# Summing a scan's states two at a time instead of four, and moving the gate multiply one scan later

## The chip, the cores and the metric

The kernel runs on one core of a Trainium2 chip. The metric is the device time of one execution in microseconds (us). The engines named below work from queues of their own and in order: PE (TensorE, matrix multiplies; PEld is its weight load), DVE (VectorE), ACT (ScalarE), POOL (GpSimd), and SP, which only issues DMAs.

## What is computed

The model has two layers over 8 sequences of 1024 positions with 256 features. The first is a mixture of experts, causal attention, and the mixture again. The second is a channel mix, a selective state-space scan, and the channel mix again. The change lies in the scan, cut here to what matters (512 inner channels `d`, 16 states `n`):

```
deltaA   = exp(delta * A)                       # [b, d, t, n]
deltaB_u = delta * B * u                        # [b, d, t, n]
state[t] = deltaA[t] * state[t-1] + deltaB_u[t]
y[t]     = sum over n of state[t, n] * C[t, n]
y        = (y + u * D) * silu(z)
out      = y @ out_proj.T + x
```

## The kernel before

The first layer ends at about 2920 us; from there to about 5470 us the scans of the second layer run (method `run` of class `Layer1`).

**Scans.** A tile has 128 partitions: 16 channels by 8 states. So one scan covers 16 channels, 8 of the 16 states and all 1024 positions. A sequence takes 64 scans: four blocks `c` of 128 channels, and in each block 8 groups of 16 channels (`l`), each in two halves `p` of the states. `order` lists all 512 scans; the main loop takes one in each turn, `i` counts them, and `k = i % 16` is the place in the block. The groups `l` are taken in the order 0, 2, 4, 6, 1, 3, 5, 7.

**One turn of the loop.** ACT makes the decays of the next scan into the tile `h` (L1648, `decay`), from data that SP's DMAs have spread over the states (`sdl`, L1616). POOL makes the input of the scan after the next (L1639, `feed`). DVE runs the scan (L1740), then multiplies by C into a tile `hc` (L1745). There are two buffers of `h`, so the decays of scan i+1 wait until `hc` of scan i-1 is made.

**The sum over states.** `add_up` lets PE sum over the 8 states of each channel, by multiplying `hc` with a matrix `pick` of zeros and ones (L1665). One group of 16 channels fills 16 columns; `pick` has 32 columns, so that two groups share a strip of 32 output partitions of the PSUM tile `y`. Consecutive groups in the order above lie in different strips: group `l` goes to strip `l // 2`. One scan takes two matmul instructions, one for each half of the positions (`t0`). `add_up` is called before scans 4, 8, 12, ... and takes the four `hc` tiles that have gathered: two groups, in two strips, with both halves of the states each. Inside a call the order is by `t0`, then by half `p`, then by scan.

**The end of a block.** In turn k = 1 of the next block `close` lets DVE add `u * D` to `y` (L1676, the tile `uc`) and POOL multiply by silu(z) (L1679, the tile `zs`). There is one `y` tile, so the first `add_up` of a block waits until L1676 has read the last one.

**Side work.** Between the scans, `side.turn(0.5)` is called twice a turn, and each call takes steps from generators by due times that are worked out when the program is built: `steps_before` (layer norm, channel mix, input projection and convolution of the next sequence), `steps_low` and `steps_delta`, `steps_gate` (silu(z)), and `steps_behind` (output projection and channel mix of the sequence before). Their matmuls are `tr` (L1228), `pk` (L1264), `pr` (L1286), `pv` (L1304), `pc` (L1391), `px` (L1421), `pu` (L1442), `pd` (L1459) and `pp` (L1524). ACT and DVE take the results out of PSUM in the same queues in which the decays and scans stand. The order on every engine is fixed by the order of the calls.

Of the kernel before, what the change touches and what calls it, by code (L numbers as in the profile page):

```python
# [40 lines left out]
NS = 16  # L41
# [1020 lines left out]
class Layer1:  # L1062
# [10 lines left out]
    NP = 8  # L1073
    G = P // NP
    PARTS = NS // NP
    Q = 4
    RG = 32
    AHEAD = 4

# [517 lines left out]
    def run(self, pools, load, load_x, keep_x, store):  # L1597
        net, nc = self.net, self.net.nc
        T, W, B = net.T, self.W, net.B
        seqs = [self.Sequence(b) for b in range(B)]  # L1600

        lines = [l for j in range(self.RG // self.G)
                 for l in range(j, P // self.G, self.RG // self.G)]
        order = [
            (b, c, l, p) for b in range(B) for c in range(NDC) for l in lines
            for p in range(self.PARTS)
        ]
        spread, inputs, decays, summed = {}, {}, {}, []

        def fetch(i):  # L1610

            if i < len(order):
                b, c, l, p = order[i]
                for name, src in (("dl", seqs[b].steps[c]), ("du", seqs[b].du[c])):
                    spread[name, i] = t = pools["s" + name].tile([P, T], F32, name="s" + name)
                    nc.sync.dma_start(  # L1616
                        t,
                        src[l * self.G : (l + 1) * self.G, :].unsqueeze(1).to_broadcast(
                            [self.G, self.NP, T]
                        ),  # L1620
                    )

        def rep(b, name, p):

            t = seqs[b].rep[name, p] = pools["rep"].tile([P, T], F32, name=f"{name}{p}")
            src = seqs[b].bc["bc".index(name)][p * self.NP : (p + 1) * self.NP, :]
            nc.sync.dma_start(t, src.unsqueeze(0).to_broadcast([self.G, self.NP, T]))

        def feed(i):


            if i < len(order):
                b, c, l, p = order[i]
                t = spread["du", i - p]
                inputs[i] = (
                    spread.pop(("du", i - p)) if p == self.PARTS - 1
                    else pools["dbu"].tile([P, T], F32, name="dbu")
                )
                nc.gpsimd.tensor_tensor(inputs[i], t, seqs[b].rep["b", p], ALU.mult)  # L1639
                if (c, l) == (NDC - 1, lines[-1]) and b + 1 < B:  # L1640
                    rep(b + 1, "b", p)

        def decay(i):
            if i < len(order):
                b, c, l, p = order[i]
                n = c * P // self.G + l
                decays[i] = pools["h"].tile([P, T], F32, name="h")
                nc.scalar.activation(  # L1648
                    decays[i], spread["dl", i - p], AF.Exp, scale=self.A[:, p, n : n + 1]
                )  # L1650

        def add_up():

            i0 = summed[0][0]
            b, c, _, _ = order[i0]
            first = i0 % NS == 0
            if first:
                self.py = pools["y"].tile([P, T], F32, name="y")
            for t0 in range(0, T, W):
                for p in range(self.PARTS):  # L1660
                    for i, hc in summed:
                        l, n = order[i][2:]
                        if n == p:
                            g, j = divmod(l, self.RG // self.G)
                            nc.tensor.matmul(  # L1665
                                self.py[g * self.RG : (g + 1) * self.RG, t0 : t0 + W],
                                self.pick[:, j, :], hc[:, t0 : t0 + W], start=(j == 0 and p == 0),
                                stop=(j == self.RG // self.G - 1 and p == self.PARTS - 1),
                            )
            summed.clear()  # L1670

        def close(i):

            b, c = order[i][:2]
            q = seqs[b]
            nc.vector.scalar_tensor_tensor(  # L1676
                q.uc[c], q.uc[c], self.skip[:, c : c + 1], self.py, ALU.mult, ALU.add
            )
            nc.gpsimd.tensor_tensor(q.uc[c], q.uc[c], q.zs, ALU.mult)  # L1679

        def before(b):

            q = seqs[b]
            q.room = (lambda: seqs[b - 2].out) if b > 1 else None
            return self.steps_before(
                q, pools, pipe, lambda x: load(x, b), lambda x: keep_x(x, b)
            )

        def behind(b):
            when = (lambda: seqs[b + 2].mixed) if b + 2 < B else None  # L1690
            return self.steps_behind(
                seqs[b], pools, pipe, lambda x: load_x(x, b), lambda x: store(x, b), when
            )

        self.tables()
        side, pipe = self.Steps(), self.Pipe()
        side.add("2before", before(0))
        side.drain("2before")
        side.add("2low", self.steps_low(seqs[0], pools, pipe))
        side.drain("2low")  # L1700
        for p in range(self.PARTS):
            rep(0, "b", p)
            rep(0, "c", p)
        for i in range(0, self.AHEAD, self.PARTS):
            fetch(i)
        feed(0)
        feed(1)
        decay(0)
        for i, (b, c, l, p) in enumerate(order):
            k = i % NS  # L1710
            if k == 2:
                if c == 0:
                    if b > 0:
                        side.drain("3behind")
                        side.add("3behind", behind(b - 1), 85, 56)
                    if b + 1 < B:
                        side.add("2before", before(b + 1), 175, 48)
            if k == (0 if 0 < c < NDC - 1 else 2):
                side.add(
                    "1gate", self.steps_gate(seqs[b], c, pools, pipe),  # L1720
                    *((30, 8) if c + 1 < NDC else (8, 2)),
                )
            if c == NDC - 1 and b + 1 < B and not seqs[b + 1].low:
                if k == 5:
                    side.drain("2before")
                if "2before" not in side.lists:
                    seqs[b + 1].low = True
                    side.add("2low", self.steps_low(seqs[b + 1], pools, pipe), 33, 6)
            if k == NS - self.AHEAD:
                side.drain("1gate")  # L1730
                if c == NDC - 1:
                    side.drain("2low")
            if p == 0:
                fetch(i + self.AHEAD)
            decay(i + 1)
            feed(i + 2)
            side.turn(0.5)
            if i % self.Q == 0 and i:
                add_up()
            nc.vector.tensor_tensor_scan(  # L1740
                decays[i], decays[i], inputs.pop(i), 0.0, ALU.mult, ALU.add
            )
            side.turn(0.5)
            hc = pools["hc"].tile([P, T], F32, name="hc")
            nc.vector.tensor_tensor(hc, decays.pop(i), seqs[b].rep["c", p], ALU.mult)  # L1745
            summed.append((i, hc))
            if (c, l) == (NDC - 1, lines[-1]) and b + 1 < B:
                rep(b + 1, "c", p)
            if k == 1:
                if i > 1:  # L1750
                    close(i - 2)
        side.drain("3behind")
        add_up()
        close(len(order) - 1)
        side.add("3behind", behind(B - 1))
        side.drain("3behind")

# [181 lines left out]
```

## Time and profile before

Three runs took 5544.22 to 5549.63 us, with a median of 5545.22 us.

| what | value |
|---|---|
| the profiled execution's own time | 5545.59 us |
| its span, first to last instruction | 5543.9 us |
| mean granted clock of TensorE over the span | 0.881 of full speed |
| stretch of the scans | 2924 to 5470 us, 2546 us |
| in that stretch, busy: PE | 1933.35 us |
| DVE | 1925.97 us |
| POOL | 1749.66 us |
| ACT | 1435.67 us |
| in that stretch, matmuls of `y` on PE | 674.99 us, 2048 records |

A group of the profile is all instructions of one line with one engine and one pair of tiles. Its busy time counts overlapping instructions once, and the mean counts each with its full length; where they overlap, the count times the mean is more than the busy time. A matmul of 32-bit numbers leaves two records in the trace[...].

### The profile page before, as it was taken

The page shows a single profiled execution, that of the slowest core. Times are in us where ns is not written, and L with a number is a line of the kernel's source. Part 1 is how long each engine was busy: PE and PEld are TensorE (multiplying, and loading weights), DVE is VectorE, ACT ScalarE, POOL GpSimd, SP SyncE. Part 2 cuts the span into 40 slices and gives each one's busy share as a digit, 9 for nine tenths or more (in the row PEclk, how much of TensorE's full clock was granted, in tenths as well). Part 3 has the DMA queues.
Part 4 walks back from the last instruction along what each step waited for, and adds up shares of the span by engine and source line. Part 5 has one row for each costly group of instructions (what it writes and reads, how often), then busy time and mean ns, then how long its engine had stood idle before and what let it go on. Part 6 is the DMA issues. An engine that isn't in the chain of part 4 may idle for free.

```text
span 5543.9 us, 60312 instructions
## 1 busy us (share of the span) xinstructions
PE 4501.1 (81%) x21046; PEld 2165.4 (39%) x21046; DVE 3400.8 (61%) x5590; ACT 2562.0 (46%) x4374; POOL 2388.7 (43%) x2089
## 2 busy tenths in 40 slices
PE   5699699999999998499766768788787778877767
PEld 5365434444444443265432233233333324333224
DVE  5632166666666764633107777778777777777884
ACT  2111145665566554011145646565564655646453
POOL 1244211111111111234317767667666766667773
PEclk6799889999999998699887889889898888989878
DMA  6133212212221221132205454535446464454652
GB/s 213 28 59 63 76 42 75 72 60 70 83 72 62 69 75 57 48 58 57 42 28 148 130 151 126 153 103 153 133 115 160 113 165 111 121 149 129 164 138 63
DMA packets 253570, 545.28 MB, mean 98 GB/s; under 512 B 30257, under 2 KB 144001, under 8 KB 253266
## 3 DMA queue, kind: packets, MB, share of 16 engines
q1 hardware_dynamic: 228690, 507.34, 33.1%
q0 software_dynamic: 24576, 34.10, 3.8%
q8 instruction: 166, 2.72, 0.2%
q14 instruction: 138, 1.13, 0.1%
HBM read 400.31 MB, written 141.03 MB: 98 GB/s over the span
## 4 chain that ended last, share of the span: by engine, by line
PE 23%; DVE 9%; ACT 7%; POOL 6%; issue 5%; DMA 3%; SPq 0%; DVEq 0%; POOLq 0%; ACTq 0%
DVE h L1740 6%; PE y L1665 4%; PE pc L1391 4%; PE pk L1264 3%; PE pr L1286 3%; PE pu L1442 2%; ACT h L1648 2%; DMA sdu<-du 1%; PE pp L1524 1%; POOL dbu L1639 1%; PE po L489 1%; DVE hc L1745 1%; PE px L1421 1%; ACT xn L1220 1%; PE pm L472 1%
## 5 line engine op out<-in xcount | busy, mean ns | idle before, releaser
L777 ACT ACTIVATE pT<-s 128x512 f32<-128x512 f32 (+3 forms) x1536 | 669.5, 489 | 522.9 <-PE s L734 513.7
L1665 PE MATMUL y<-hc,pick 128*32 128x512 f32 x2048 | 675.0, 739 | 280.4 <-DVE hc L1745 269.1
L734 PE MATMUL s<-kT,qT 32*128 32x512 f32 (+3 forms) x3072 | 829.9, 538 | 14.1 <-DVE mx L750 11.4
L1648 ACT ACTIVATE h<-sdl,A 128x1024 f32<-128x1024 f32 x512 | 567.6, 1113 | 510.8 <-DVE hc L1745 490.6
L1740 DVE TENSOR_TENSOR_SCAN h<-h,dbu 128x1024 f32<-128x1024 f32 x256 | 586.5, 2291 | 283.1 <-ACT h L1648 161.5
L734 PE MATMUL s<-qT,kT 32*128 32x512 f32 (+3 forms) x3072 | 743.4, 539 | 8.1 <-ACT pT L777 8.1
L1639 POOL TENSOR_TENSOR dbu<-sdu,b 128x1024 f32<-128x1024 f32 x256 | 602.5, 2354 | 284.6 <-DVE h L1740 142.0
L1740 DVE TENSOR_TENSOR_SCAN h<-h,sdu 128x1024 f32<-128x1024 f32 x256 | 586.4, 2290 | 186.6 <-ACT h L1648 149.0
L1745 DVE TENSOR_TENSOR hc<-h,c 128x1024 f32<-128x1024 f32 x512 | 626.0, 1223 | 48.1 <-DMA c<-bc 9.7
L783 POOL TENSOR_SCALAR_AFFINE_SELECT pT<-pT 128x512 f32<-128x512 f32 x256 | 162.4, 634 | 1136.5 <-ACT pT L777 1052.8
L1639 POOL TENSOR_TENSOR sdu<-sdu,b 128x1024 f32<-128x1024 f32 x256 | 602.4, 2353 | 14.8 <-DMA b<-bc 2.8
L734 PEld LDWEIGHTS s<-kT,qT 32*128 32x128 f32 x3072 | 319.6, 186 | 434.9 <-DVE mx L750 188.6
L476 ACT ACTIVATE mid<-pm,bu 128x512 f32<-128x512 f32 x192 | 131.6, 686 | 728.8 <-PE pm L472 721.3
L747 DVE TENSOR_REDUCE part<-s 128x1 f32<-128x512 f32 x512 | 329.2, 685 | 178.5 <-PE s L734 177.9
L1665 PEld LDWEIGHTS y<-hc,pick 128*32 128x32 f32 x2048 | 133.5, 127 | 774.8 <-DVE hc L1745 386.7
L497 POOL DMA_INDIRECT acc<-o,idx x128 | 210.5, 1644 | 495.5 <-DVE o L494 240.6
L750 DVE CUSTOM_DVE_ANT_0 junk<-s,mask,part 128x256 f32<-128x256 f32 (+3 forms) x512 | 281.5, 550 | 157.5 <-PE s L734 112.6
L472 PE MATMUL pm<-tT,wu 128*128 128x512 f32 x768 | 362.4, 609 | 0.0
L489 PE MATMUL po<-wd,mid 128*128 128x256 f32 x1536 | 350.4, 392 | 0.0
L750 DVE CUSTOM_DVE_ANT_0 junk<-s,mask 128x256 f32<-128x256 f32 (+3 forms) x512 | 250.5, 489 | 138.9 <-PE s L734 86.7
L797 PE MATMUL po<-pT,at_v 128*32 128x512 f32 (+3 forms) x3072 | 329.5, 501 | 0.7 <-POOL pT L783 0.4
L1442 PE MATMUL pu<-hT,w_in 128*128 128x512 f32 x512 | 269.1, 667 | 63.7 <-DVE cm_r L1310 48.7
(261 smaller groups left out, 6778.8 us busy)
## 6 DMA issues: line engine op xcount, KB each, us to landing
sdl<-dl SPq DMA_DIRECT2D x256, 512.0 KB
sdu<-du SPq DMA_DIRECT2D x256, 512.0 KB
acc<-xt SPq DMA_DIRECT2D x24, 1024.0 KB
xt<-acc SPq DMA_DIRECT2D x24, 1024.0 KB
rows<-moe_r SPq DMA_DIRECT2D x16, 1056.0 KB
qT<-padded_q SPq DMA_DIRECT2D x32, 512.0 KB
kT<-padded_k SPq DMA_DIRECT2D x32, 512.0 KB
kept<-so SPq DMA_DIRECT2D x64, 256.0 KB
```

The costliest lines, as they stand in the source:

```text
L472: nc.tensor.matmul(pm, wu[:, k, n * P : (n + 1) * P], tT[:, k, t0 : t0 + HALF], start=(k == 0), stop=(k == KC - 1),)
L489: nc.tensor.matmul(po, mid[:, n, j * P : (j + 1) * P], wd[:, n, :], start=(n == 0), stop=(n == NF - 1),)
L734: self.net.nc.tensor.matmul(s[:, 0 : rhs.shape[-1]], lhsT, rhs, start=True, stop=True)
L750: nc.vector.tensor_tensor_reduce(junk[:, 0:w], sh[:, 0:w], self.mask[:, W - w : W], 1.0, part if a else -3e38, ALU.add, ALU.max, self.mx[n ...
L777: self.net.nc.scalar.activation(pT[:, h, 0:w], sh[:, 0:w], AF.Exp, scale=1.0 / HD**0.5)
L797: nc.tensor.matmul(q.po[h * HS : (h + 1) * HS, o:W], self.va[q.b % 2][:, j, g * HG + h, :], pT[:, h, 0 : W - o], start=(j == 0), stop=(j = ...
L1442: self.net.nc.tensor.matmul(pu, self.w_in[:, k, e0 : e0 + P], q.hT[:, k, t0 : t0 + self.W], start=(k == 0), stop=(k == KC - 1),)
L1639: nc.gpsimd.tensor_tensor(inputs[i], t, seqs[b].rep["b", p], ALU.mult)
L1648: nc.scalar.activation(decays[i], spread["dl", i - p], AF.Exp, scale=self.A[:, p, n : n + 1])
L1665: nc.tensor.matmul(self.py[g * self.RG : (g + 1) * self.RG, t0 : t0 + W], self.pick[:, j, :], hc[:, t0 : t0 + W], start=(j == 0 and p == 0 ...
L1740: nc.vector.tensor_tensor_scan(decays[i], decays[i], inputs.pop(i), 0.0, ALU.mult, ALU.add)
L1745: nc.vector.tensor_tensor(hc, decays.pop(i), seqs[b].rep["c", p], ALU.mult)
```

## The change

`Q` goes from 4 to 2, so `add_up` is called at every second scan and takes the two halves `p` of one group of channels, which lie in one strip. The call stands after the scan instead of ahead of it. The multiply by silu(z) leaves `close` for a function `gated`, which is called in turn k = 2, behind the next `feed`.

```diff
-    Q = 4
+    Q = 2
...
-            i0 = summed[0][0]
-            b, c, _, _ = order[i0]
-            first = i0 % NS == 0
-            if first:
+            if summed[0][0] % NS == 0:
                 self.py = pools["y"].tile([P, T], F32, name="y")
...
+
+        def gated(i):
+            b, c = order[i][:2]
+            q = seqs[b]
             nc.gpsimd.tensor_tensor(q.uc[c], q.uc[c], q.zs, ALU.mult)
...
             feed(i + 2)
+            if k == 2 and i > NS:
+                gated(i - 3)
             side.turn(0.5)
-            if i % self.Q == 0 and i:
-                add_up()
             nc.vector.tensor_tensor_scan(
                 decays[i], decays[i], inputs.pop(i), 0.0, ALU.mult, ALU.add
             )
+            if i % self.Q == 0 and i:
+                add_up()
             side.turn(0.5)
...
         close(len(order) - 1)
+        gated(len(order) - 1)
```

## The prediction

> **What bounds the kernel.** I read the page's chain first, then the groups, and then only the stretch of the scans, by windows of four scans. The chain for the whole span:
>
> ```profile
> PE 23%; DVE 9%; ACT 7%; POOL 6%; issue 5%; DMA 3%; SPq 0%; DVEq 0%; POOLq 0%; ACTq 0%
> L1665 PE MATMUL y<-hc,pick 128*32 128x512 f32 x2048 | 675.0, 739 | 280.4 <-DVE hc L1745 269.1
> L1740 DVE TENSOR_TENSOR_SCAN h<-h,dbu 128x1024 f32<-128x1024 f32 x256 | 586.5, 2291 | 283.1 <-ACT h L1648 161.5
> ```
>
> PE leads the chain. The sums are PE's largest group of the scan stretch, and the scans themselves wait for ACT's decays, which stand in ACT's queue behind work that takes results from PE. So a late PE becomes a late scan by way of ACT.
>
> The sequences 1 to 6 repeat each other within a few us. I take sequence 3 (3871.3 to 4202.4 us) as the pattern. Six of its 16 windows (bounds and length; then busy time and count of PE, PEld, DVE, ACT, POOL; clock; DMA share and rate):
>
> ```profile
> 3871.30:3891.70 20.40, 13.68 (x29) 2.59 (x30) 17.17 (x19) 9.86 (x13) 13.60 (x7) 0.67 0.97 248
> 3930.30:3950.40 20.10, 20.10 (x79) 12.34 (x77) 13.95 (x10) 10.85 (x13) 9.44 (x4) 1.00 0.34 91
> 4048.10:4077.80 29.70, 26.62 (x86) 12.72 (x84) 15.17 (x9) 20.05 (x29) 12.15 (x12) 1.00 0.23 59
> 4097.10:4113.50 16.40, 16.40 (x57) 7.70 (x54) 14.45 (x10) 10.59 (x15) 12.00 (x7) 1.00 0.56 147
> 4130.50:4153.10 22.60, 22.29 (x60) 8.39 (x59) 15.19 (x9) 13.62 (x15) 10.62 (x6) 1.00 0.20 50
> 4173.00:4187.60 14.60, 9.25 (x24) 2.63 (x24) 13.76 (x9) 5.49 (x7) 14.44 (x9) 0.73 0.57 170
> ```
>
> Four scans need 14 us of DVE (4 x (2.29 + 1.22)). The last row is near that, and the first is filled by DVE (17.17 us) and the DMAs (share 0.97): there PE has room. In the four between, PE is busy 90 to 100% and the scans are stretched: there PE is the bound. The chain of this sequence, in order of weight, begins:
>
> ```profile
> by line: PE y L1665 10.2%; PE pc L1391 8.5%; DMA sdu<-du 7.8%; DVE h L1740 7.7%; issue 6.8%; PE pk L1264 6.8%; PE pr L1286 6.4%; PE pu L1442 4.9%; ACT h L1648 4.3%; PE pp L1524 3.9%; ACT L1156 2.3%; DMA c<-bc 2.3%; PE px L1421 2.2%; POOL db
> ```
>
> 10.2% of 331.1 us are 33.8 us of `y` on the path.
>
> **What a sum costs, paired and alone.** One call of `add_up` before, from the timeline (start, length, engine, line):
>
> ```profile
> 3599.78 3.63 PE L1665 MATMUL y<-hc,pick 128*32 128x512 f32 x16
> ...
> 3600.24 0.12 PEld L1665 LDWEIGHTS y<-hc,pick 128*32 128x32 f32 x2 [0.31 <-issue]
> 3600.66 0.12 PEld L1665 LDWEIGHTS y<-hc,pick 128*32 128x32 f32 x2 [0.31 <-issue]
> 3601.09 0.12 PEld L1665 LDWEIGHTS y<-hc,pick 128*32 128x32 f32 x2 [0.31 <-issue]
> ```
>
> 16 records (8 instructions[...]) take 3.63 us, and the weights come two at a time every 0.43 us: two matmuls run beside each other, one in the strip of each group. Alone they show where one group's second half is ready and the other's is not:
>
> ```profile
> 3835.55 0.11 PEld L1665 LDWEIGHTS y<-hc,pick 128*32 128x32 f32 x1 [0.31 <-issue]
> 3835.97 0.11 PEld L1665 LDWEIGHTS y<-hc,pick 128*32 128x32 f32 x1 [0.32 <-issue]
> ...
> 3842.01 0.19 PEld L1665 LDWEIGHTS y<-hc,pick 128*32 128x32 f32 x4 [5.92 <-DVE hc L1745]
> ```
>
> One load instead of two, at the same step of 0.42 us. A lone record costs as much as a pair. The full-width neighbour agrees: `pk` (128 columns, 512 positions) takes 3.60 us for 8 records, one after the other.
>
> With Q = 2 a call holds the two halves of one group, in one strip, adding into the same partitions: nothing is left to run beside. Each call has 4 instructions, 8 records, 8 x 0.43 = 3.43 us. Four scans then cost 6.87 us of PE instead of 3.43 us of steps. **PE gains 3.43 us of work per four scans**; x128 that is 439 us at full clock.
>
> Here a rule speaks against the change. The Trainium skill (TensorE: Matmul & The Clock Gate, Part 3, and the table "Why this matters for your kernels") says to put small-M outputs in different strips of 32 partitions so that they run concurrently, and gives 2.38x for three tiles. Scaled evenly, two tiles would gain 1.59x and losing them would cost 3.63 x 0.59 = 2.1 us per four scans, in all 274 us of PE. The row of this trace has twice the work in the same step, so I take 3.43 us and 439 us.
>
> **Part by part.**
>
> *Call behind the scan.* The call emits only PE work. The order on DVE, ACT and SP does not change; on PE the order of the side work does not either. The call stays between the same two side turns, so its move past a DVE instruction alone is worth 0. The wait is still for `hc` of scan i-1, not for scan i. If it took in scan i, the price would be up to 2.29 us in a call; I see no reason for it.
>
> *Every second scan.* In turns i = 4, 8, ... PE has a group at the same place as before, with 8 lone steps instead of 8 paired ones: 0. In turns i = 2, 6, ... there is a new group of 3.43 us between pieces of side work, which now waits for the `hc` before it. Behind it stand side matmuls, and behind these ACT's evacuations and the decays. Where PE is late, the wait is over already; where PE is early, DVE is the bound and has its inputs. Between 0 and 3.43 us per window at full clock, so I go through the windows of sequence 3 by what stands behind the new group:
>
> - Windows 1, 15, 16 (from 3871, 4173, 4188 us; DVE and DMAs bound, PE idle 5.4 to 6.7 us): 0. Window 3 (3930): the new group comes behind `pr`, whose result ACT waits for: 0 there. Window 7 (4012): only an empty gap: 0.
> - Window 2 (3892): the group falls between the transposes and `pp`, for which DVE waits 13 us: 3.4. Window 4 (3950): late by the group of window 3, `pv` comes later than DVE's read of it, which had about 0.6 us to spare: 2.8. Window 6 (3991): the group of window 5 splits `pr`, ACT's sigmoid is late, a scan waits for ACT already: 2.2. Window 8 (4028): between transposes, with `y` on the path already: 3.4.
> - Windows 9, 10, 11, 13, 14 (PE 76 to 100% busy, `pc`, `pr` or `px` behind the group): 3.4, 3.0, 3.4, 3.4, 3.4. Window 12 (PE idle 4.2 us, half usable): 2.0.
> - Window 5: -1.0 for the gate, next.
>
> Sum: 29.4 us a sequence, x6 = 176 us.
>
> *Gate multiply later.* In POOL's queue L1679 moves behind one `feed`:
>
> ```profile
> POOL uc L1679 <- DVE uc L1676: 268.9, 30, 18.6
> ```
>
> POOL stood 269 us before this multiply in total. It now feeds first. But the inputs are made two scans ahead, and POOL is idle over 30% of the stretch; on the path lie only 2.35 us, in window 5, beside an ACT branch (`pk`, `ka`, decays) nearly as long. The gain lies between 0 and 2.35 us a sequence: I take 1.0. The tile `zs` is next written some 6 scans later and `uc` is read by `pp` from turn 5, so nothing waits for the later gate.
>
> *One `y` tile.* A block's first sum moves from k = 4 to k = 2, right behind L1676 (1.28 us). Where PE has nothing else it waits up to 1.28 us; that is window 5 and its like, inside the 2.2 above.
>
> *Changes between strip and full width.* 128 more groups; the step from the last `y` to a full-width matmul is 0.52 instead of 0.43 us. 128 x 0.1 x two sides, half of it hidden: about 10 us, left inside the rounding of the windows.
>
> *Sequences 0 and 7.* Their chains carry 20.7 us (7.1% of 291.8) and 18.4 us (6.8% of 271) of `y`. By the ratio to 33.8, sequence 0 gives 29.4 x 20.7 / 33.8 = 18 us. Of sequence 7, 4.3 us are the last call, whose 8 steps stay 8, and most windows are bound by DVE (33.3% of its chain are scans): 8 us.
>
> **Sum: 176 + 18 + 8 = 202 us.** On the profiled execution's 5545.6 us that gives 5748 us; that execution is 0.4 us above the median of the runs, so the same holds for the median.
>
> **Rivals.**
>
> *A. PE becomes the bound everywhere.* For: PE 1933 us busy of 2546, plus 439 at a mean clock of 0.86 = 510, is 2443 of 2546, and side work that can't run ahead four scans leaves gaps. If the extra can't fill idle time at all: 5546 + 439 = 5985 us. Against: PE's idle time (73 us a sequence) lies to a third in windows bound by DVE or DMA. 14%.
>
> *B. Most is hidden.* More PE work also holds the clock up: the granted clock is 0.67 to 0.86 in windows with PE idle, and 31% of the `y` records run at half clock (mean 739 ns between 592 and 1063). Warm instead of cold saves 0.43 us a step. With half the windows absorbed: 5545 + 100 = 5645 us. 13%.
>
> *C. Faster.* The mechanism is POOL's blocked queue: if the 269 us before the gate hold back the inputs, freeing them brings 2.35 us plus a wait of up to 8.5 us in each block, and sums that come two scans sooner fill PE's idle 73 us a sequence. It decides if the 55 us of extra a sequence (16 x 3.43) fit the idle time wholly. About -30 us: 5515 us. Against: the windows with PE at 100%. 7%.
>
> *D. No difference,* if the two strips did not in fact run beside each other. The paired loads exclude it: 2%.
>
> **Numbers.** Forecast 64%. Its own range is 5665 to 5840 us: below, four windows of a sequence absorbed (-13 x 6); above, the whole chain share doubled plus gaps (49 us a sequence in place of 34). With the near part of B, and A reaching down, 5640 to 5870 us holds the time 8 times in 10. Under 0.2% (11 us) a measurement of this kernel can't tell from no change. Slower 0.91, same 0.02, faster 0.07.
>
> **What will show it.** Right: `y` records still 2048, but busy near 1000 us or more instead of 675, single loads every 0.43 us, the windows from 4028 to 4173 us longer by some 3 us each, and POOL's wait before L1679 gone. Wrong: `y` busy time unchanged (D), DVE-bound windows grown as much as the others (A), or the PE-bound windows not grown (B, C).

## The result, and the profile after

The changed kernel took 5647.7 us (median of 4 runs, 5642.7 to 5651.8), against 5547.43 us for the kernel before on the same chip: 100 us more, a ratio of 1.0179 with a 95% interval of 1.0167 to 1.0192. The forecast was 202 us more. The sign was right, the loss half of what was expected.

The chain of the page of the kernel after, by engine and by line:

```profile
PE 32%; DVE 7%; ACT 4%; issue 4%; POOL 3%; DMA 3%; SPq 0%; DVEq 0%; POOLq 0%; ACTq 0%
PE y L1662 10%; DVE h L1741 5%; PE pr L1286 4%; PE pc L1391 4%; PE pk L1264 3%; PE pu L1442 3%; PE pp L1524 2%; DMA sdu<-du 1%; PE po L489 1%; ACT h L1648 1%; PE pv L1304 1%; PE px L1421 1%; PE pm L472 1%; DVE hc L1748 1%; ACT xn L1220 1%
```

PE's share of the chain rose from 23 to 32%. The row of `y` in the costliest groups of the same page (L1665 is now L1662):

```profile
L1662 PE MATMUL y<-hc,pick 128*32 128x512 f32 x2048 | 1018.4, 663 | 196.1 <-DVE hc L1748 179.9
```

The count is the same, and the busy time is 343 us higher. So the pairs are gone, as the forecast said. But the time grew by only 100 us. Four windows of sequence 3 after (columns as in the prediction) show where the rest went; they answer to the windows from 4048, 4097, 4131 and 4173 us before:

```profile
4100.50:4132.00 31.50, 31.50 (x88) 13.84 (x86) 15.19 (x10) 20.27 (x30) 12.62 (x13) 1.00 0.20 53
4151.20:4169.40 18.20, 18.20 (x46) 6.84 (x45) 14.43 (x10) 10.67 (x15) 11.68 (x7) 1.00 0.48 127
4185.80:4210.20 24.40, 24.09 (x56) 8.87 (x56) 15.20 (x10) 13.63 (x15) 11.36 (x6) 1.00 0.18 47
4233.80:4248.40 14.60, 11.78 (x24) 3.36 (x24) 13.77 (x9) 5.48 (x7) 14.44 (x9) 0.77 0.57 172
```

The last window is as long as before, and there the sums are hidden, as forecast. In the first, PE does 4.9 us more and the window is 1.8 us longer; PE's idle time there fell from 3.1 us to nothing. Windows are counted from 1 in each sequence, and the four above are numbers 9, 11, 13 and 15. Mean change of length over sequences 1 to 6, beside what the prediction charged (us; each window is four scans):

| window | 1 | 2 | 3 | 4 | 5 | 6 | 7 | 8 | 9 | 10 | 11 | 12 | 13 | 14 | 15, 16 | sum |
|---|---|---|---|---|---|---|---|---|---|---|---|---|---|---|---|---|
| predicted | 0 | 3.4 | 0 | 2.8 | -1.0 | 2.2 | 0 | 3.4 | 3.4 | 3.0 | 3.4 | 2.0 | 3.4 | 3.4 | 0 | 29.4 |
| measured | -0.3 | 3.2 | 0 | 3.1 | -1.2 | 0 | 3.7 | -1.7 | 1.8 | 0 | 1.8 | -0.6 | 1.8 | 3.7 | -0.1 | 15.1 |

Windows 9 to 13 were charged 15.2 us and took 4.8. The five together in sequence 3, before and after:

```profile
4048.10:4153.10 105.00, 94.38 (x271) 39.55 (x270) 73.07 (x44) 68.82 (x94) 66.58 (x46) 0.98 0.43 113
4100.50:4210.20 109.70, 109.39 (x271) 42.22 (x270) 73.03 (x45) 68.90 (x94) 66.66 (x46) 1.00 0.40 107
```

PE is busy 15.0 us longer, about what was charged: `y` takes 18.1 us more (19.2 to 37.3 us), PE's other matmuls 3.1 us less. But PE's idle time falls by 10.3 us, from 10.6 to 0.3, and 15.0 - 10.3 = 4.7. PE's waits in these five windows, from the list of waits of the kernel before (engine, line and releaser; us in total, times, longest):

```profile
PE pc L1391 <- ACT tap L1383: 4.7, 3, 1.7
PE pu L1442 <- DVE cm_r L1310: 2.5, 1, 2.5
PE pu L1442 <- ACT zs L1509: 1.7, 1, 1.7
PE y L1665 <- DVE hc L1745: 1.5, 1, 1.5
PE px L1421 <- ACT zs L1509: 0.3, 1, 0.3
```

The same list of the kernel after, over the same five windows, has one entry:

```profile
PE px L1421 <- ACT zs L1509: 0.3, 1, 0.3
```

The sum falls from 10.7 to 0.3 us. PE's timeline shows how. Before (start, length, work, and in brackets the idle time ahead of it):

```profile
4051.51 7.11 PE L1391 MATMUL pc<-u,tap 128*128 128x512 f32 x16 [1.73 <-ACT tap L1383]
...
4088.86 3.60 PE L1442 MATMUL pu<-hT,w_in 128*128 128x512 f32 x8
4094.14 1.98 PE L1442 MATMUL pu<-hT,w_in 128*128 128x512 f32 x4 [1.68 <-ACT zs L1509]
...
4119.85 3.43 PE L1442 MATMUL pu<-hT,w_in 128*128 128x512 f32 x4 [2.46 <-DVE cm_r L1310]
...
4128.70 7.11 PE L1391 MATMUL pc<-u,tap 128*128 128x512 f32 x16 [1.73 <-ACT tap L1383]
```

After, at the same places of PE's queue:

```profile
4102.11 3.62 PE L1662 MATMUL y<-hc,pick 128*32 128x512 f32 x8
4105.66 7.14 PE L1391 MATMUL pc<-u,tap 128*128 128x512 f32 x16
...
4151.98 3.62 PE L1662 MATMUL y<-hc,pick 128*32 128x512 f32 x8
4155.53 1.98 PE L1442 MATMUL pu<-hT,w_in 128*128 128x512 f32 x4
...
4171.52 3.62 PE L1662 MATMUL y<-hc,pick 128*32 128x512 f32 x8
4175.07 3.70 PE L1442 MATMUL pu<-hT,w_in 128*128 128x512 f32 x8
...
4182.20 3.62 PE L1662 MATMUL y<-hc,pick 128*32 128x512 f32 x8
4185.75 7.14 PE L1391 MATMUL pc<-u,tap 128*128 128x512 f32 x16
```

The new calls stand just ahead of matmuls that had waited for ACT or DVE, and these no longer wait. Behind the longest of the waits the matmuls had also run slowly (4 records of `pu` in 3.43 us, against 8 in 3.70 us after): that is half of the 3.1 us. A call of 8 records takes 3.62 us, as the whole call of 16 did: the lone step is as forecast.

### The profile page after: what moved, and what is told of

It reads as the page before. It is cut to its first block, busy times and chain, and to the rows that moved or that the text cites. A ratio compares the mean times of both kernels' runs of the same rounds, so it can differ in the third digit from the quotient of the medians.

```text
span 5643.3 us, 60293 instructions
## 1 busy us (share of the span) xinstructions
PE 4815.3 (85%) x21046; PEld 2235.0 (40%) x21046; DVE 3402.2 (60%) x5590; ACT 2563.1 (45%) x4374; POOL 2387.2 (42%) x2089
## 4 chain that ended last, share of the span: by engine, by line
PE 32%; DVE 7%; ACT 4%; issue 4%; POOL 3%; DMA 3%; SPq 0%; DVEq 0%; POOLq 0%; ACTq 0%
PE y L1662 10%; DVE h L1741 5%; PE pr L1286 4%; PE pc L1391 4%; PE pk L1264 3%; PE pu L1442 3%; PE pp L1524 2%; DMA sdu<-du 1%; PE po L489 1%; ACT h L1648 1%; PE pv L1304 1%; PE px L1421 1%; PE pm L472 1%; DVE hc L1748 1%; ACT xn L1220 1%
## 5 line engine op out<-in xcount | busy, mean ns | idle before, releaser
L1662 PE MATMUL y<-hc,pick 128*32 128x512 f32 x2048 | 1018.4, 663 | 196.1 <-DVE hc L1748 179.9
L1748 DVE TENSOR_TENSOR hc<-h,c 128x1024 f32<-128x1024 f32 x512 | 626.1, 1223 | 42.3 <-DMA c<-bc 8.1
L1662 PEld LDWEIGHTS y<-hc,pick 128*32 128x32 f32 x2048 | 213.7, 119 | 922.3 <-issue 605.3
L489 PEld LDWEIGHTS po<-wd,mid 128*128 128x128 f32 x1536 | 303.0, 198 | 44.4 <-issue 1.0
```

What stands on the lines that cost most here:

```text
L489: nc.tensor.matmul(po, mid[:, n, j * P : (j + 1) * P], wd[:, n, :], start=(n == 0), stop=(n == NF - 1),)
L1662: nc.tensor.matmul(self.py[g * self.RG : (g + 1) * self.RG, t0 : t0 + W], self.pick[:, j, :], hc[:, t0 : t0 + W], start=(j == 0 and p == 0 ...
```

## The experiments

The question was where the missing 100 us are: in waits that the new calls fill because of where they stand, in the gate multiply, in a warmer clock, or in the pairing itself. "Theory F" and "theory P" below name the first. The edits are cut to the lines that matter, and `...` marks what is left out. "More" is against the median of the kernel before in the same set of runs.

**The gate alone.** L1679 moved as in the change, `Q` still 4:

```diff
+        def gated(i):
...
+            if k == 2 and i > NS:
+                gated(i - 3)
             side.turn(0.5)
...
```

> The kernel before with the gate multiply alone moved behind the next feed; sums still of four scans. Theory F (the lone sums cost 439 us of PE, and all but some 100 us of it fill time in which PE waited anyway): the gate is a small matter, 5530 to 5548 us. Theory G (the lone sums do cost some 200 us, and the gate multiply gives 100 us of it back, since POOL stood 269 us before it): about 5450 us.

5535.8 us, 8.7 us less (ratio 0.9987, 0.9977 to 0.9996). The gate gives back a little, 2 to 13 us by the interval, and not 100. It doesn't do so in window 5, where the prediction expected it: that window is 0.1 us shorter in the mean. In the change window 5 is 1.2 us shorter, and with Q alone (below), where the gate is as before, it is too.

**Half a sum.** The changed kernel with the first half of the states left out of `y`:

```diff
-                for p in range(self.PARTS):
+                for p in range(1, self.PARTS):
...
```

> The changed kernel, with the sum taken over the second half p of the states alone, so that half of the matmuls of y is left out: each call is 2 instructions instead of 4, and per four scans PE does what the pairs did before (3.43 us of steps), while the calls still come at every second scan and still wait for the last hc. Theory F (the cost is the lost pairing): back to the kernel before, 5520 to 5552 us. Rival W (the cost is the new wait at every second scan and the shorter run ahead of PE): stays at 5600 us or more.

5470.08 us, 74 us less than the kernel before (ratio 0.9867, 0.985 to 0.9883), outside both expectations. With as many steps as the kernel before, but in twice as many calls, it is clearly faster. So new waits at every second scan are not what costs (rival W falls), and the calls between are worth something in themselves.

**Half a sum more.** The changed kernel with the second half added twice:

```diff
-                for p in range(self.PARTS):
+                for p, again in ((0, 0), (1, 0), (1, 1)):
...
```

> The changed kernel, with the second half p of the states added twice, so that y is too large: 6 instructions a call instead of 4, again 3.43 us more of PE per four scans, 439 us in all at full clock. Theory F: the waits of PE between 4100 and 4186 us of sequence 3 are used up (PE idle 0.3 us of 109.6 in the changed kernel), so windows 9 to 14 now grow by nearly 3.4 us each, where the first step gave them 1.4 on average; in all 170 to 260 us more than the changed kernel, 5820 to 5910 us. Theory C (the clock: more work keeps PE warm and pays for half of what is added): about 100 us again, 5730 to 5770 us.

5878.91 us: 231 us more than the changed kernel, for another 439 us at full clock, spread over the old and the new calls. Windows 9 to 14 grew by a further 20.4 us of the 20.6 (6 x 3.43) added. There PE's idle time was already spent. A warmer clock that pays for half (theory C) would have given about 100 us again.

**The pairing alone, at the old places.** The kernel before, its call summed group by group:

```diff
-            for t0 in range(0, T, W):
-                for p in range(self.PARTS):
+            for own, t0, p in [
+                (own, t0, p) for own in sorted({order[i][2] for i, _ in summed})
+                for t0 in range(0, T, W) for p in range(self.PARTS)
+            ]:
...
-                        if n == p:
+                        if n == p and l == own:
...
```

> The kernel before, with the four scans of a call summed group by group, so that neighbours in PE's queue go to the same strip: the lost pairing alone, in a lump at the old place, with no new call and the gate as before. Theory F with place (the new groups stand ahead of matmuls that wait for ACT or DVE and fill these waits, a lump at the old place does so less): 5670 to 5740 us. Theory F by amount only (any place fills PE's idle time): 5640 to 5660 us. If the pairs were not what was lost: 5545 us.

5638.93 us, 94 us more (ratio 1.0168, 1.0151 to 1.0185). The size of the added work was not what the expectation assumed, so neither theory is decided by this. A call, from PE's timeline of this run:

```profile
3685.34 5.37 PE L1668 MATMUL y<-hc,pick 128*32 128x512 f32 x16
```

5.37 us for 16 records are 12 steps of 0.43 us and the tail, not 16: where one group ends and the next begins, four records of each still run side by side (the starts are four steps alone, four in pairs, four alone). So this run adds only 4 x 0.43 = 1.72 us per four scans, 220 us in all, and loses 94 us to it.

**Q alone.** The kernel before with one line changed:

```diff
-    Q = 4
+    Q = 2
```

> The kernel before with Q = 2 alone: the call still ahead of the scan, the gate multiply still in close. Theory F: the call's place against the scan is worth 0 and the gate little, so 5645 to 5665 us, at most 15 us above the changed kernel. Theory G (the gate gives back 100 us): about 5750 us.

5652.22 us, 107.5 us more (ratio 1.0196, 1.0173 to 1.0219): the change without the gate. The call's place ahead of or behind the scan is worth nothing that these runs can tell.

**Split pairs.** Two calls per four scans, each with one half of both groups, so that the strips stay side by side (`add_up` now takes the half that it is to sum, and leaves the rest for later):

```diff
+        def add_up(half=None):
...
-            if i % self.Q == 0 and i:
-                add_up()
+            if i % 4 == 3:
+                add_up(0)
+            if i % 4 == 0 and i:
+                add_up(1)
```

> The changed kernel, but in each four scans the first halves p of the two groups are summed after the third scan and the second halves after the fourth: two calls per four scans as in the change, each with two strips side by side. Theory F: PE does what it did before, in two pieces of 1.72 us, 5520 to 5550 us, perhaps a little faster than the kernel before since less stands behind the last hc. Rival W (more calls cost by their waits): 5570 us or more.

5494.2 us, 50.5 us less than the kernel before (ratio 0.991, 0.9887 to 0.9934): more than expected. It beats both kernels with everything computed. Its row of `y` in the page:

```profile
L1664 PE MATMUL y<-hc,pick 128*32 128x512 f32 x2048 | 636.7, 681 | 268.8 <-DVE hc L1752 254.9
```

The busy time is not above that of the kernel before (675.0 us), so the pairs are kept.

**The same PE work at the old places.** This run was made for the question that the pairing run left open. In the kernel before, every pair is issued twice, so that `y` comes out doubled:

```diff
-                for p in range(self.PARTS):
+                for p, new, last in ((0, 1, 0), (0, 0, 0), (1, 0, 0), (1, 0, 1)):
...
```

> The kernel before with every pair of matmuls of y issued twice, so that y comes out doubled: 16 steps a call in place of 8, 3.43 us more per four scans, all of it in the calls at the old places and none between; the gate as before. It adds the same PE work as the change, 439 us at full clock. Theory P (the place of the work decides: half a call of lone work at the old places cost 12 us a sequence, and a second half costs more since the idle time is used): 30 to 45 us a sequence, 5740 to 5830 us. Theory N (place is nothing, PE's idle time takes what it can): as the changed kernel, 5645 to 5670 us.

5766.51 us, 218.5 us more (ratio 1.0388, 1.0365 to 1.041). A call, from PE's timeline of this run:

```profile
3657.98 7.06 PE L1665 MATMUL y<-hc,pick 128*32 128x512 f32 x32
```

7.06 us instead of 3.63: the 3.43 us per four scans that the change adds too. A sequence grew by 29.8 us, and windows 9, 11, 13 and 14 by 3.4 us each. The same steps of PE cost 218.5 us at the old places and 107.5 us where Q alone puts them (both with the gate as before). The clock doesn't tell the two apart: the profiled executions show 0.906 and 0.904. The waits do. Windows 9 to 13 of sequence 3 grew by 11.0 us here and by 4.7 with Q alone, at a clock of 1.00 in both. With Q alone the list of PE's waits there is down to the one entry of 0.3 us, and here it still says:

```profile
PE pc L1391 <- ACT tap L1383: 3.5, 2, 1.7
PE pu L1442 <- ACT zs L1509: 1.7, 1, 1.7
PE y L1665 <- DVE hc L1745: 0.7, 1, 0.7
PE px L1421 <- ACT zs L1509: 0.3, 1, 0.3
```

In the whole of sequence 3 PE's idle time fell from 73.8 us to 60.2 here and to 50.0 with Q alone. That is 10 of the 14 us between the two; the other 4 us are steps that ran faster with Q alone.

**Later calls.** Split pairs, with the second halves one scan later:

```diff
-            if i % 4 == 0 and i:
+            if i % 4 == 1 and i > 1:
                 add_up(1)
```

> The run with split pairs, but the second halves are summed one scan later, so that the calls stand two scans apart and neither needs the hc of the last scan. Theory P (a call is cheap where nothing that ACT waits for stands behind it, and where its hc tiles are long ready): 5470 to 5495 us, at or under the split pairs. If the last call of a block, now behind scan k = 1, holds up DVE's read of y in each block (1 to 2 us in 32 blocks): 5525 to 5560 us.

5545.0 us, no different from the kernel before (ratio 0.9992, 0.9982 to 1.0002). Most of what the split had gained is lost. DVE's wait before L1676, from the list of waits of the kernel before and of this run (over the scans):

```profile
DVE uc L1676 <- PE y L1665: 82.0, 23, 7.2
```

```profile
DVE uc L1675 <- PE y L1664: 151.3, 22, 14.2
```

It rose to 151 us; with the split pairs it was 62.3 us. A run that keeps the late call except at the end of a block tells whether that is the reason:

```diff
-            if i % 4 == 0 and i:
+            if (k == 0 and i) or (i % 4 == 1 and k > 1):
                 add_up(1)
```

> The run with split pairs, its second halves one scan later as in the late run, except at the end of a block, where they stay at k = 0 so that DVE's read of y isn't held up. Theory P, if the late run lost only at the block ends: at or under the split pairs, 5475 to 5500 us. If a call that waits for an older hc brings nothing by itself: 5490 to 5510 us, the split pairs again. If the late calls cost elsewhere too: 5520 us or more.

5503.25 us, 40.5 us less than the kernel before (ratio 0.9923, 0.9906 to 0.994). DVE's wait before L1675 is back at 62.6 us. The block ends were the reason, and a call that waits for an older `hc` brings nothing more.

**The sum of the runs.** Steps of 0.43 us at full clock, by where they stand (old: the calls at every fourth scan; new: the calls between), without the gate's 8.7 us:

| run | at old places | at new places | measured | per us of PE |
|---|---|---|---|---|
| pairing alone | +220 us | 0 | +94 us | 0.43 |
| pairs issued twice | +439 us | 0 | +218.5 us | 0.50 |
| Q alone | 0 | +439 us | +107.5 us | 0.24 |
| split pairs | -220 us | +220 us | -50.5 + 8.7 = -42 us | see below |

If work at the old places is worth 0.43 and at the new places 0.24, the split should give 220 x (0.24 - 0.43) = -42 us. It gave that, but the fit is partly luck. The half sum moves as many steps and comes to -66 us without the gate. The late calls leave no steps at the old places, or one call in four, so by the same prices they should have gained more than the split pairs; they come to +6 us (late) and -32 us (late except at block ends). So the two prices hold for the change on average, and the exact turn of a call matters as much. The new calls of the half sum stand one turn earlier than those of the split pairs; whether its further 24 us come from that stays open.

## Where the prediction was right, and the step that failed

**Right.** The lost pairing, the step of 0.43 us, the old calls unchanged in length (8 lone steps for 8 paired), and the 439 us of added PE work at full clock. The estimate scaled from the 2.38x of the Trainium skill (TensorE: Matmul & The Clock Gate, Part 3), 2.1 us per four scans, was further off: the timeline shows twice the work in the same step. The call's place against the scan: 0, as forecast. Windows 1 to 4 and 14 to 16 came within 0.4 us.

**Right by luck.** The gate: a gain of 6 us (1.0 us in six sequences) was taken and 8.7 us were measured. But POOL's wait before the multiply is still there for the most part (173 of 269 us), against what the prediction said would show it right, and window 5 got shorter without the gate. And the measured time, 5647.7 us, lies within the outer range of 5640 to 5870 us, though at its edge and for a loss half of the forecast.

**Wrong.** The step that failed is the charge for "the new group of 3.43 us" in windows 6 to 13 of a sequence, above all "Windows 9, 10, 11, 13, 14 (PE 76 to 100% busy, `pc`, `pr` or `px` behind the group): 3.4, 3.0, 3.4, 3.4, 3.4" and 2.0 for window 12. The reasoning went from a high busy share, and from what stands behind the group, to the whole group lengthening the window. But PE still waited 10.7 us for ACT and DVE in windows 9 to 13, and the new calls stand in front of the instructions that waited. They took the place of the waits; 10.4 us of these vanished, and 4.8 us were paid instead of 15.2.

Windows 6 to 8 were charged 5.6 us and took 2.0. Of these, window 6 was charged 2.2 us and took nothing, and its row before shows why it couldn't be PE's: DVE is busy in 20.80 of its 20.90 us.

```profile
3991.00:4011.90 20.90, 11.82 (x30) 5.19 (x30) 20.80 (x39) 11.44 (x15) 18.09 (x15) 0.82 0.52 151
```

Windows 7 (charged 0, took 3.7) and 8 (charged 3.4, took -1.7) were wrong both ways; why stays open. In all a sequence was charged 29.4 us and took 15.1. Doubled pairs at the old places cost almost that charge, 29.8 us, but in other windows (2 took nothing there, 3 and 7 over 3 us each), so the agreement is chance.

Sequences 0 and 7, scaled from the same sum to 18 and 8 us, came to 6.8 and -5.7 us. By the two profiles this makes 92 us from the first scan on. The first scan starts 7.8 us later in the profile after, though the change leaves all that comes ahead of it as it was; over all eleven profiles it starts between 2916.9 and 2930.7 us, so a few us between two executions tell nothing.

Rival B ("most is hidden") named the size, 5645 us, and its reason, the clock, has a part. The clock in the scans rose from 0.86 to 0.91. PE's sums are busy 343 us longer and its other work 35 us shorter (1258 to 1223 us), so the 439 us at full clock became 308 us of busy time. But windows 9 to 13, where the charge failed most, ran at 0.98 before and 1.00 after: there 10.3 us went into waits, and at most 3.1 us can be the clock's. A further step of the same work cost 231 us instead of 100, though the clock rose again, to 0.94. No run held the clock fixed, so its share of the rest isn't separated. Rival A (no hiding) and rival C (faster) both fell; of C's idea that POOL's queue held back the inputs, the gate's 8.7 us are the most that can be left.

## What to carry to other kernels

Work added to an engine that works in order is priced by its place in the queue, not only by the engine's busy share: ahead of an instruction that waits for another engine it can cost half or nothing (1.8 us or less of 3.43 in windows 9 to 13), ahead of one that another engine waits for it can cost its full length (3.4 us of 3.43 in four windows with the pairs doubled). So list the waits of the bounding engine, and look at which instruction the new work stands in front of. When small matmuls are cut into smaller calls, keep in each call the ones that use different strips: the cut with its pairs kept gained 42 us here (50.5 less the gate's 8.7), and the cut that lost the pairs cost 107.5 us.

## What the runs showed of the hardware

Two matmuls of different strips need not be issued as neighbours one by one: when four instructions of one strip were followed by four of another, 16 records still took 12 steps instead of 16 (5.37 us a call), since the end of one group ran beside the start of the next.
